# Delta rule: a head's values turned to tokens by VectorE in 32x32 blocks and a DRAM round trip, in place of TensorE transposes

## The chip, the cores and the metric

The kernel runs on one core of a Trainium2 chip. A core has five engines, each with an instruction queue of its own that it works through in order: TensorE (PE in the profile; its weight loads are PEld), VectorE (DVE), ScalarE (ACT), GpSimd (POOL) and SyncE (SP), which here does nothing but issue DMAs. Engines wait for one another through semaphores. The metric is the time of one execution on the device, in microseconds; the median of three runs is given, beside one execution that was taken with the profiler.

## The reference, cut to what matters

The program is a decoder block of three parts: a gated delta rule (16 heads of 128 channels), a cross-attention and an attention with a mixture of experts. Only the delta rule is touched. For 4 sequences of 512 tokens:

```python
q = _causal_conv(x @ Wq.T, cw_q, cb_q)        # 4 taps along the tokens, then silu
k = _causal_conv(x @ Wk.T, cw_k, cb_k)
v = _causal_conv(x @ Wv.T, cw_v, cb_v)
...
q = _l2norm(q.reshape(Bb, Ss, H, DK))
k = _l2norm(k.reshape(Bb, Ss, H, DK))
v = v.reshape(Bb, Ss, H, DV)

def step(Sstate, inputs):
    q_t, k_t, v_t, g_t, beta_t = inputs
    retrieved = jnp.einsum('bhkv,bhk->bhv', Sstate, k_t)
    error = v_t - g_t[..., None] * retrieved
    update = k_t[..., :, None] * (beta_t[..., None] * error)[..., None, :]
    Snew = g_t[..., None, None] * Sstate + update
    o_t = jnp.einsum('bhkv,bhk->bhv', Snew, q_t)
    return (Snew, o_t)
...
o = o * jax.lax.rsqrt(jnp.mean(o * o, axis=-1, keepdims=True) + EPS) * norm_w
o = o * jax.nn.silu(x @ Wg.T)
return o @ Wo.T
```

The kernel computes the scan in chunks of 128 tokens: inside a chunk a triangular matrix is inverted, and between chunks a state of 128x128 is carried.

## The kernel before, in words

The delta rule works on 32 *pairs* `m`: a sequence `b` (4 of them) and two of its heads (`HG = 2`, index `p`), 64 heads in all. All data is float32. Each pair goes through three stages, and the stages of neighbouring pairs are woven together.

- `stage1(m)` makes keys and queries. `conv` (L598 to L612) multiplies a weight by the normalized input on PE into a PSUM tile `pb` (channels in the rows, 512 tokens in the columns), then one ACT pass (L606) and three DVE passes (L609) make the convolution in a tile `cv`, and ACT's SiLU ends it (L612). For a gate (`m == 3`) there is only the SiLU, into a tile `gs` (L602). `stage1` also writes the triangular matrices to DRAM (`at_d`, L675), and reads them back as blocks (`iA`, L740).
- `stage2_inverse(m)` inverts the blocks on POOL (on DVE for the first two pairs), 62 instructions (L751, L752), and takes the result through DRAM (`t_d`, L759; `x_d`, L762) into tiles `T` and `X` (L767, L768).
- `stage2_values(m)` makes the values and the gates. For each head it runs `conv`; PE transposes the four 128x128 chunks into a PSUM tile (L799), so that tokens are in the rows; DVE multiplies by the token's factor `nr` into the tile `vn` (L801, four buffers). Beside the first head, POOL raises `rq` to a power (L804, L805) and SP writes it to DRAM (L806).
- `stage3(m)` completes the inverse (L847 to L881), then goes through the four chunks: state times keys (L899, PE), `r` = values minus the decayed product (L901, DVE, reads `v_[p]`), inverse times `r` (L908, PE; in chunk 0 the values themselves), `u` (L910, ACT), the new state (L918 PE, L923 DVE), the output (L926, L928). Then `og` (L939) multiplies the output by norm weight and gate on DVE and frees the gate's buffer.
- `output(m)` multiplies by `Wo` (L972).

The order of work is written with Python generators. A generator yields at the points where others may go on. For pair `m`, each step of `stage3(m)` is followed by one *turn* of the rest:

```python
rest.append((stage1(m + 2), 2))
...
rest.append((stage2_values(m + 1), 1))
rest.append((inversions(m, turn), 2))
...
rest = turns(*rest)
for _ in stage3(m):
    next(rest, None)
```

A turn is thus two steps of `stage1(m + 2)`, one of `stage2_values(m + 1)`, two of the inversion, and one of `output`. A head of `stage2_values` takes five steps for its values, and two for its gate; 14 in all.

DVE, ACT and POOL issue in the order in which the program traces them (`manual_schedule`). PE's and SP's order is fixed at compile time by a planner that goes by its own estimates of when each instruction will be ready. At run time every queue, SP's too, is in order: a DMA that waits holds all that stand behind it.

Of the kernel before, what the change touches and what calls it, by code (L numbers as in the profile page):

```python
# [31 lines left out]
F32 = mybir.dt.float32  # L32
BF16 = mybir.dt.bfloat16
AF = mybir.ActivationFunctionType
ALU = mybir.AluOpType
# [4 lines left out]
P = 128  # L40
B, S, D = 4, 512, 512
NT = B * S // P
TB = S // P
# [3 lines left out]
HG = 2  # L47
# [57 lines left out]
def decoder(ctx: ExitStack, tc: tile.TileContext, a: dict, out: bass.AP):  # L105
    nc = tc.nc
# [6 lines left out]
    ident = tab[:, C_ID, :]  # L113
# [3 lines left out]
    mhalf = const.tile([P, 64], F32, name="mhalf")  # L117
# [5 lines left out]
    def along(ap, n):  # L123

        return ap.unsqueeze(2).to_broadcast([P, ap.shape[1], n])
# [22 lines left out]
    def chain(*gs):  # L148
        for g in gs:
            yield from g  # L150
# [31 lines left out]
    def run(*gs):  # L182
        for g in gs:
            for _ in g:
                pass
# [17 lines left out]
    dram = ctx.enter_context(tc.tile_pool(name="dram", bufs=1, space=DRAM))  # L203
# [174 lines left out]
    with ExitStack() as st:  # L378
# [3 lines left out]
        w2 = st.enter_context(tc.tile_pool(name="a_2", bufs=2))  # L382
# [14 lines left out]
        p_b = st.enter_context(tc.tile_pool(name="a_pb", bufs=4, space=PSUM))  # L397
# [23 lines left out]
        SLOTS = 3  # L421
# [3 lines left out]
        r_d = [dram.tile([HG * TB, P], F32, name=f"r_d{n}") for n in range(SLOTS)]  # L425
# [21 lines left out]
        def blocks(d):  # L447

            f = d.rearrange("c x -> (c x)").rearrange("(n x) -> n x", x=BLK)
            return f[:, : 32 * P].rearrange("n (r t) -> n r t", r=32)[:, :, 0:32]  # L450
# [133 lines left out]
        def load_weights(m, *what, by=nc.sync):  # L584

            for n in what:
                if m < B * NHG:
                    t = (s1 if n < 2 else s2).tile([P, KD, HG * P], F32, name=f"w{n}", bufs=1)
                    by.dma_start(t, a["a_w"][m % NHG][:, n])
                    weights[m, n] = t  # L590

        def conv(b, hg, p, m, wt, dst):

            h = hg * HG + p
            xnT = seqs[b][0]
            pj = p_b.tile([P, S], F32, name="pb")
            for kd in range(KD):
                nc.tensor.matmul(pj, wt[:, kd, p * P : (p + 1) * P], xnT[:, kd, :], start=kd == 0, stop=kd == KD - 1)  # L598
                if kd == 1:
                    yield  # L600
            if m == 3:
                nc.scalar.activation(dst, pj, AF.Silu)  # L602
                yield
                return
            ac = w2.tile([P, S], F32, name="cv", bufs=5)
            nc.scalar.activation(ac, pj, AF.Identity, bias=cb[:, m, h : h + 1], scale=cw[:, m, h, 3:4])  # L606
            yield
            for j in range(1, 4):
                nc.vector.scalar_tensor_tensor(ac[:, j:], pj[:, : S - j], cw[:, m, h, 3 - j : 4 - j], ac[:, j:], ALU.mult, ALU.add)  # L609
                if j == 2:  # L610
                    yield
            nc.scalar.activation(ac if dst is None else dst, ac, AF.Silu)  # L612
            return ac
# [174 lines left out]
        def stage2_values(m):  # L788

            b, hg = divmod(m, NHG)  # L790
            nr, rq = keys[m][4:]
            wv, wg = weights.pop((m, 2)), weights.pop((m, 3))
            v_, gs = [], []
            for p in range(HG):
                t = yield from conv(b, hg, p, 2, wv, None)
                yield
                tp = p_b.tile([P, TB, P], F32, name="pb")
                for c in range(TB):
                    nc.tensor.transpose(tp[:, c, :], t[:, c * P : (c + 1) * P], ident)  # L799
                v = w2.tile([P, TB, P], F32, name="vn", bufs=4)  # L800
                nc.vector.tensor_tensor(v, tp, along(nr[:, p * TB : (p + 1) * TB], P), ALU.mult)  # L801
                v_.append(v)
                if p == 0:
                    nc.gpsimd.tensor_scalar(rq, rq, 1e-24, None, ALU.max)  # L804
                    nc.gpsimd.tensor_tensor(rq, rq, mhalf[:, 0 : HG * TB], ALU.pow)  # L805
                    nc.sync.dma_start(r_d[m % SLOTS].rearrange("c t -> (c t)").rearrange("(n k) -> n k", k=HG * TB), rq)  # L806
                yield
            load_weights(m + 1, 2)
            for p in range(HG):
                g = w2.tile([P, S], F32, name="gs", bufs=3)  # L810
                yield from conv(b, hg, p, 3, wg, g)
                gs.append(g)
            load_weights(m + 1, 3)
            pairs[m] = (v_, gs)

# [17 lines left out]
        def stage3(m):  # L833

            b, hg = divmod(m, NHG)
            xnT, beta, gam, ngam, gend, gall = seqs[b]
            kT, kd_, qg, pt, _, _ = keys.pop(m)
            Ts, Xs, ats = joined.pop(m)
            v_, gs = pairs.pop(m)
# [44 lines left out]
            t = w2.tile([P, HG, S], F32, name="rrow", bufs=1)  # L884
# [5 lines left out]
            for c in range(TB):  # L890
                cs = slice(c * P, (c + 1) * P)
                rs = []
                for p in range(HG):
                    h = hg * HG + p
                    if c == 0:
                        rs.append(v_[p][:, 0, :])
                        continue
                    pk = p_s.tile([P, P], F32, name="ps")
                    nc.tensor.matmul(pk, kT[p][:, cs], st_[p], start=True, stop=True)  # L899
                    r = small.tile([P, P], F32, name="r", bufs=3)  # L900
                    nc.vector.scalar_tensor_tensor(r, pk, ngam[:, h, c : c + 1], v_[p][:, c, :], ALU.mult, ALU.add)  # L901
                    rs.append(r)
                if c:
                    yield
                us = []
                for p in range(HG):
                    pu = p_s.tile([P, P], F32, name="ps")
                    nc.tensor.matmul(pu, Xs[p][:, c, :], rs[p], start=True, stop=True)  # L908
                    u = small.tile([P, P], F32, name="u", bufs=4)
                    nc.scalar.copy(u, pu)  # L910
                    us.append(u)
                yield
                nst = list(st_)
                for p in range(HG):
                    h = hg * HG + p
                    if c < TB - 1:
                        pn = p_s.tile([P, P], F32, name="ps")
                        nc.tensor.matmul(pn, kd_[p][:, c, :], us[p], start=True, stop=True)  # L918
                        s_ = small.tile([P, P], F32, name="state", bufs=4)
                        if c == 0:  # L920
                            nc.scalar.copy(s_, pn)
                        else:
                            nc.vector.scalar_tensor_tensor(s_, st_[p], gall[:, h, c : c + 1], pn, ALU.mult, ALU.add)  # L923
                        nst[p] = s_
                for p in range(HG):
                    nc.tensor.matmul(po[p][:, c, :], us[p], pt[p][:, c, :], start=True, stop=c == 0)  # L926
                    if c > 0:
                        nc.tensor.matmul(po[p][:, c, :], st_[p], qg[p][:, cs], start=False, stop=True)  # L928
                st_ = nst
                if 0 < c <= HG:  # L930
                    nc.gpsimd.tensor_tensor(gs[c - 1], gs[c - 1], rb[c - 1], ALU.mult)
                yield
# [150 lines left out]

        context = prepare()
        run(turns((stage2_inverse(0), 2), (chain(pair0, turns((stage1(1), 2), (stage2_values(0), 1))), 1), (itertools.islice(context, 11), 1)))
        begun[1] = stage2_inverse(1)
        for m in range(NP):
# [29 lines left out]
            if m + 1 < NP:  # L1117
                rest.append((stage2_values(m + 1), 1))
                rest.append((inversions(m, turn), 2))
# [8 lines left out]
            for _ in stage3(m):  # L1128
                next(rest, None)
# [12 lines left out]
    with ExitStack() as st:  # L1142
        keep = st.enter_context(tc.tile_pool(name="b_keep", bufs=1, reuse_waits="tile"))
        small = st.enter_context(tc.tile_pool(name="b_small", bufs=4, reuse_waits="tile"))
        p_b = st.enter_context(tc.tile_pool(name="b_pb", bufs=6, space=PSUM, reuse_waits="tile"))
# [571 lines left out]
        for i in range(NT - 1):  # L1717
            g, kind = rest_of(i), "rest_of"
            if i in (3, 7, 11):
                g, kind = chain(g, route(i - 3, 4)), "route"  # L1720
                at_e.append((i + 1.6, 2.0 if i < 11 else 0.45, enter(i - 3), "enter"))
            elif i == NT - 4:
                g, kind = chain(g, table(EARLY, "e", count, None, True, ahead)), "route"
            elif i == NT - 2:
                g, kind = chain(g, route(12, 3)), "route"
# [179 lines left out]
```

## Time and profile before

| what | value |
|---|---|
| three runs | 3327.7, 3330.07, 3330.5 us |
| median | 3330.07 us |
| the profiled execution | 3329.88 us |
| its span, first to last instruction | 3328.1 us |
| mean granted TensorE clock | 0.981 |
| instructions | 48186 |
| DMA | 476.09 MB, mean 143 GB/s |
| the delta rule's values (L801) | from 103 to 1788 us |

The span is what the trace covers; 1.8 us lie around it. A group of the profile reads: line, engine, operation, what it writes and reads with buffer numbers left out, shapes, count, then busy time in us and the mean of one in ns, then the idle time of the engine just before these instructions and what ended it. The busy time counts overlapping instructions once; the mean of one does not, so a pipelined matmul's mean is longer than the time for which it holds the engine. Two records stand for one float32 matmul, one for a float32 transpose. In a timeline, `SPq` is the issue of a DMA on SP, whose length is the issue's, not the transfer's.

### The profile page before, as it was taken

Reading aid. Unit: us, or ns where it says so; the run is one execution under the profiler, and the core shown is the slowest. Engines: PE = TensorE matmul, PEld = TensorE weight load, DVE = VectorE, ACT = ScalarE, POOL = GpSimd, SP = SyncE. Lnnn points to the kernel's source line nnn. Section 1 sums busy time; section 2 is a strip of 40 time slices with the busy share of each in tenths; the row PEclk is TensorE's granted clock in tenths of the full one; section 3 lists DMA queues with packets and bytes.
Section 4 is the critical chain, followed back from the end, with each engine's and each line's share of the span. In section 5 each row is a group of like instructions: output and inputs, shape, how many; then the busy total and the mean of one; then the engine's idle time right before and its main releaser. Section 6 shows DMA issues by size and latency. Waiting matters only on the chain. (4 is left out here: it accounts for less than half of the span.)

```text
span 3328.1 us, 48186 instructions
## 1 busy us (share of the span) xinstructions
PE 3166.4 (95%) x16015; PEld 1775.2 (53%) x16015; DVE 1831.9 (55%) x4184; ACT 1606.6 (48%) x4391; POOL 1465.7 (44%) x2780
## 2 busy tenths in 40 slices
PE   5899999999999999999998789999999999999998
PEld 3555555555555555555555445555555555555444
DVE  5665555546555556555454566656665665646211
ACT  3445555545554455545453346455555555645222
POOL 1156757676666666676765211112212221121443
PEclk8999999999999999999998799999999999999999
DMA  6343534444444434454434455556655565567454
GB/s 171 103 134 114 145 103 131 138 124 126 118 129 137 133 117 121 124 148 126 121 108 120 144 178 185 176 161 186 183 167 165 184 168 155 175 198 263 93 89 60
DMA packets 491032, 476.09 MB, mean 143 GB/s; under 512 B 225332, under 2 KB 340554, under 8 KB 490656
## 3 DMA queue, kind: packets, MB, share of 16 engines
q1 hardware_dynamic: 477616, 444.59, 45.5%
q0 software_dynamic: 11728, 25.58, 3.8%
q8 instruction: 128, 2.10, 0.3%
q10 hardware_dynamic: 1440, 2.84, 0.3%
q14 instruction: 120, 0.98, 0.1%
HBM read 411.23 MB, written 61.69 MB: 142 GB/s over the span
## 5 line engine op out<-in xcount | busy, mean ns | idle before, releaser
L598 PE MATMUL pb<-xnT,w 128*128 128x512 f32 x2048 | 958.6, 603 | 0.5 <-DVE at L674 0.2
L598 PEld LDWEIGHTS pb<-xnT,w 128*128 128x128 f32 x2048 | 364.8, 192 | 340.4 <-issue 333.5
L609 DVE SCALAR_TENSOR_TENSOR cv<-pb,pp,cv 128x510 f32<-128x510 f32 (+2 forms) x576 | 424.3, 746 | 92.7 <-ACT cv L606 79.4
L752 POOL TENSOR_TENSOR iT<-iT,iW 64x126 f32<-64x126 f32 (+22 forms) x930 | 344.7, 371 | 72.8
L1267 PE MATMUL pb<-c_q,hT 128*128 128x512 f32 x768 | 353.0, 599 | 3.3 <-DMA c_q<-in_c_wq_dram 1.6
L751 POOL TENSOR_TENSOR iW<-iA,iT 64x126 f32<-64x126 f32 (+22 forms) x930 | 321.6, 346 | 65.7 <-issue 0.2
L1186 POOL TENSOR_TENSOR rope_s<-q,tab 128x128 f32<-128x128 f32 x80 | 45.0, 563 | 481.6 <-DVE q L1297 368.3
L972 PE MATMUL pb<-wot,og 128*128 128x512 f32 x512 | 247.6, 607 | 5.5 <-DVE xa L977 4.5
L1267 PEld LDWEIGHTS pb<-c_q,hT 128*128 128x128 f32 x768 | 141.4, 192 | 157.4 <-issue 147.3
L606 ACT ACTIVATE cv<-pb,pp 128x512 f32<-128x512 f32 x192 | 148.7, 774 | 148.1 <-PE pb L598 144.2
L653 POOL TENSOR_TENSOR rk<-ss,mhalf 128x8 f32<-128x8 f32 x32 | 77.7, 2428 | 276.3 <-DVE ss L652 276.3
L977 DVE TENSOR_TENSOR xa<-pb,xa 128x512 f32<-128x512 f32 x112 | 77.1, 688 | 187.2 <-PE pb L972 187.2
L306 ACT ACTIVATE x_e<-pb,nm,x_step 128x256 f32<-128x256 f32 x256 | 141.2, 565 | 57.8 <-DVE nm L302 56.7
L1380 PE MATMUL pw<-wot,oT 128*128 128x512 f32 x344 | 162.6, 599 | 1.6 <-DVE oT L1372 1.3
L1333 PE MATMUL pb<-kT,qT 128*128 128x256 f32 (+3 forms) x576 | 163.2, 409 | 0.8 <-ACT og L1339 0.7
L705 POOL TENSOR_TENSOR qg<-qh,row 128x512 f32<-128x512 f32 x64 | 82.8, 1293 | 171.7 <-ACT qh L612 149.2
L972 PEld LDWEIGHTS pb<-wot,og 128*128 128x128 f32 x512 | 92.6, 192 | 100.2 <-issue 89.2
L612 ACT ACTIVATE qh<-cv 128x512 f32<-128x512 f32 x64 | 40.4, 631 | 212.8 <-DVE cv L609 212.8
L1782 PE MATMUL pb<-w_gu,eT 128*128 x288 | 130.3, 595 | 3.1 <-issue 3.1
L1366 ACT COPY eT<-pb 128x512 f32<-128x512 f32 x160 | 91.5, 596 | 85.2 <-PE pb L1364 84.3
L132 POOL TENSOR_TENSOR rms_r<-rsq,mhalf 128x1 f32<-128x1 f32 x48 | 27.3, 570 | 220.4 <-DVE rsq L131 220.4
L458 ACT ACTIVATE em<-em,ee 128x128 f32<-128x128 f32 x256 | 78.3, 388 | 94.5 <-POOL ee L655 81.6
(436 smaller groups left out, 6239.9 us busy)
## 6 DMA issues: line engine op xcount, KB each, us to landing
c_q<-in_c_wq_dram SPq DMA_DIRECT2D x128, 512.0 KB
w<-in_a_w_dram SPq DMA_DIRECT2D x124, 512.0 KB
wot<-in_c_wo_dram SPq DMA_DIRECT2D x86, 512.0 KB
row<-g_d SPq DMA_DIRECT2D x64, 512.0 KB
c_o<-in_c_wo_dram SPq DMA_DIRECT2D x42, 512.0 KB
at_d<-at SPq DMA_DIRECT2D x64, 256.0 KB
rrow<-r_d SPq DMA_DIRECT2D x32, 512.0 KB
T<-t_d SPq DMA_DIRECT2D x32, 512.0 KB
```

Source lines behind the costliest of these rows:

```text
L306: nc.scalar.activation(e[:, 2 * r + g, :], ps[r][:, g, :], AF.Exp, bias=nm[:, r, g : g + 1], scale=step[:, h : h + 1], accum_out=ssum[:, g ...
L598: nc.tensor.matmul(pj, wt[:, kd, p * P : (p + 1) * P], xnT[:, kd, :], start=kd == 0, stop=kd == KD - 1)
L606: nc.scalar.activation(ac, pj, AF.Identity, bias=cb[:, m, h : h + 1], scale=cw[:, m, h, 3:4])
L609: nc.vector.scalar_tensor_tensor(ac[:, j:], pj[:, : S - j], cw[:, m, h, 3 - j : 4 - j], ac[:, j:], ALU.mult, ALU.add)
L751: eng.tensor_tensor(u, A[:, i, i + 1 :].unsqueeze(2).to_broadcast([nb, n, w]), T[:, i, :w].unsqueeze(1).to_broadcast([nb, n, w]), ALU.mult)
L752: eng.tensor_tensor(T[:, i + 1 :, :w], T[:, i + 1 :, :w], u, ALU.add)
L972: nc.tensor.matmul(pw, og[p][:, c * P : (c + 1) * P], wot[:, p, :], start=p == 0, stop=p == HG - 1)
L1267: nc.tensor.matmul(pj, hT[:, kd, :], w[:, kd % 2, :], start=kd == 0, stop=kd == KD - 1)
L1333: nc.tensor.matmul(ps[:, m, k * P : (k + w) * P], qT[g][:, n + m, :], kT[:, g, j : j + w, :], start=True, stop=True)
L1366: nc.scalar.copy(eT, tp)
L1380: nc.tensor.matmul(pw, oT[:, h + m, :], w[:, m, :], start=g == 0 and h + m == 0, stop=g == 3 and h + m == 3)
L1782: nc.tensor.matmul(pg, hT[:, kd, :], w_gu[:, bass.ds(e, 1), kd, :, :], start=kd == 0, stop=kd == KD - 1)
```

## The change

The four transposes of a head on PE go, with their PSUM tile. A generator `brought` does their work for each head. VectorE transposes every 32x32 block of the head's 128x512 tile in place of its own position, so that row `32 q + j` holds token `j` of every block of 32 tokens and 32 channels of group `q`. Four DMAs, one for each group of 32 rows, write the blocks to a DRAM tile `v_d` in the order of the tokens (pieces of 512 bytes). Two turns later one DMA reads it back as the tile `vn` (2 KB a row), and two turns after that DVE multiplies it by `nr`, in place. The convolutions stand in `conv_all`, as they were, and after each of its steps the heads that have begun take one step of `brought`; the number of steps of `stage2_values` stays 14, and the second head's multiply is traced in the last of them.

The order inside `vn` is now channel group, chunk, 32 channels, so `stage3` reads a chunk of it as four pieces of 32, and `r` is written by the same instruction with its operands seen as four blocks.

```diff
-            v_, gs = [], []
-            for p in range(HG):
-                t = yield from conv(b, hg, p, 2, wv, None)
-                yield
-                tp = p_b.tile([P, TB, P], F32, name="pb")
-                for c in range(TB):
-                    nc.tensor.transpose(tp[:, c, :], t[:, c * P : (c + 1) * P], ident)
-                v = w2.tile([P, TB, P], F32, name="vn", bufs=4)
-                nc.vector.tensor_tensor(v, tp, along(nr[:, p * TB : (p + 1) * TB], P), ALU.mult)
-                v_.append(v)
...
+            v_, gs, beside = [], [], []
+
+            def brought(p, t):
+
+                x = w2.tile([P, 4, TB, 32], F32, name="vt", bufs=1)
+                nc.vector.transpose(x.rearrange("p b k i -> p k b i"), t.rearrange("p (k b j) -> p k b j", b=4, j=32))
+                d = dram.tile([P, 4, P], F32, name="v_d", bufs=4)
+                for q in range(4):
+                    nc.sync.dma_start(d[:, q, :].rearrange("(b j) x -> j b x", b=4), x[q * 32 : (q + 1) * 32].rearrange("p b k i -> p b (k i)"))
+                yield
+                yield
+                v = w2.tile([P, 4, TB, 32], F32, name="vn", bufs=4)
+                v_.append(v.rearrange("p a k i -> p k a i"))
+                nc.sync.dma_start(v.rearrange("p a k i -> p a (k i)"), d)
+                yield
+                yield
+                nc.vector.tensor_tensor(v, v, nr[:, p * TB : (p + 1) * TB].unsqueeze(1).unsqueeze(3).to_broadcast([P, 4, TB, 32]), ALU.mult)
+
+            def conv_all():
+                for p in range(HG):
+                    t = yield from conv(b, hg, p, 2, wv, None)
+                    yield
+                    beside.append(brought(p, t))
+                    if p == 0:
...
+                    yield
+                load_weights(m + 1, 2)
+                for p in range(HG):
+                    g = w2.tile([P, S], F32, name="gs", bufs=3)
+                    yield from conv(b, hg, p, 3, wg, g)
+                    gs.append(g)
+
+            for _ in conv_all():
+                for g in beside:
+                    next(g, None)
+                yield
+            run(*beside)
             load_weights(m + 1, 3)
             pairs[m] = (v_, gs)
...
-                        rs.append(v_[p][:, 0, :])
+                        rs.append(v_[p][:, 0])
...
-                    nc.vector.scalar_tensor_tensor(r, pk, ngam[:, h, c : c + 1], v_[p][:, c, :], ALU.mult, ALU.add)
+                    blocks = lambda t: t.rearrange("p (a i) -> p a i", i=32)
+                    nc.vector.scalar_tensor_tensor(blocks(r), blocks(pk), ngam[:, h, c : c + 1], v_[p][:, c], ALU.mult, ALU.add)
                     rs.append(r)
```

More of the change, by code (lines that the diff above doesn't have):

```diff
@@ L792, in stage2_values @@
             wv, wg = weights.pop((m, 2)), weights.pop((m, 3))
-            v_, gs = [], []
-            for p in range(HG):
-                t = yield from conv(b, hg, p, 2, wv, None)
-                yield
-                tp = p_b.tile([P, TB, P], F32, name="pb")
-                for c in range(TB):
-                    nc.tensor.transpose(tp[:, c, :], t[:, c * P : (c + 1) * P], ident)
-                v = w2.tile([P, TB, P], F32, name="vn", bufs=4)
-                nc.vector.tensor_tensor(v, tp, along(nr[:, p * TB : (p + 1) * TB], P), ALU.mult)
-                v_.append(v)
[L803 to L806, printed above, removed]
-                yield
@@ L808, in stage2_values @@
[L808 to L812, printed above, removed]
+            v_, gs, beside = [], [], []
[5 more added lines that the diff above has]
+                    nc.sync.dma_start(d[:, q, :].rearrange("(b j) x -> j b x", b=4), x[q * 32 : (q + 1) * 32].rearrange("p b k i -> p b (k i)"))
+                yield
+                yield
+                v = w2.tile([P, 4, TB, 32], F32, name="vn", bufs=4)
[4 more added lines that the diff above has]
+                nc.vector.tensor_tensor(v, v, nr[:, p * TB : (p + 1) * TB].unsqueeze(1).unsqueeze(3).to_broadcast([P, 4, TB, 32]), ALU.mult)
@@ new lines, in conv_all @@
+            def conv_all():
[4 more added lines that the diff above has]
+                    if p == 0:
+                        nc.gpsimd.tensor_scalar(rq, rq, 1e-24, None, ALU.max)
+                        nc.gpsimd.tensor_tensor(rq, rq, mhalf[:, 0 : HG * TB], ALU.pow)
+                        nc.sync.dma_start(r_d[m % SLOTS].rearrange("c t -> (c t)").rearrange("(n k) -> n k", k=HG * TB), rq)
+                    yield
[4 more added lines that the diff above has]
+                    gs.append(g)
```

## The prediction

> **What bounds the kernel now.** I read the page first, then the busy time by stretches, then the groups by form for the edited lines, then the timeline of one pair (from 697 to 753 us), and last who waits on SP's queue.
>
> The page, engines over the whole span:
>
> ```profile
> PE 3166.4 (95%) x16015; PEld 1775.2 (53%) x16015; DVE 1831.9 (55%) x4184; ACT 1606.6 (48%) x4391; POOL 1465.7 (44%) x2780
> ```
>
> The stretches of the delta rule's stage (columns: stretch, PE, PEld, DVE, ACT and POOL busy us with counts, granted clock, DMA share, GB/s):
>
> ```profile
> 600.00:800.00 200.00, 198.90 (x1167) 114.62 (x1165) 106.11 (x175) 100.82 (x282) 138.05 (x297) 1.00 0.48 135
> 800.00:1000.00 200.00, 196.02 (x1150) 116.07 (x1150) 117.16 (x218) 108.59 (x304) 130.54 (x279) 1.00 0.45 126
> ```
>
> From 200 to 1800 us PE is busy 97 to 99.5% at a granted clock of 1.00 (0.97 in the last stretch); DVE and ACT stand near 54%, POOL near 67%. PE sets this stage: PE time that goes comes off the end, unless another engine makes PE wait.
>
> The groups by form of the lines that go:
>
> ```profile
> L799 PE MATMUL pb<-tab,cv 128*128 128x128 f32 x256 | 42.8, 291 | 3.6 <-ACT cv L612 3.6
> L801 DVE TENSOR_TENSOR vn<-pb,nr 128x512 f32<-128x512 f32 x64 | 44.2, 691 | 72.1 <-PE pb L799 72.1
> ```
>
> The timeline around the second head's values of one pair (start, length):
>
> ```profile
> 715.55 0.60 DVE L901 SCALAR_TENSOR_TENSOR r<-ps,ngam,vn 128x128 f32<-128x128 f32 x2
> 716.27 0.61 ACT L612 ACTIVATE cv<-cv 128x512 f32<-128x512 f32 x1
> 716.94 0.66 PE L799 MATMUL pb<-tab,cv 128*128 128x128 f32 x4
> 717.43 0.61 PE L908 MATMUL ps<-r,X 128*128 128x128 f32 x4
> 717.63 0.69 DVE L801 TENSOR_TENSOR vn<-pb,nr 128x512 f32<-128x512 f32 x1 [1.48 <-PE pb L799]
> 719.02 0.92 SPq L759 DMA_DIRECT2D t_d<-iT  x2
> 721.93 0.38 SPq L767 DMA_DIRECT2D T<-t_d  x1
> 723.06 0.36 SPq L768 DMA_DIRECT2D X<-x_d  x1
> 725.08 1.17 SPq L724 DMA_DIRECT2D rq<-sr  x2
> 726.19 0.69 DVE L688 TENSOR_TENSOR pt<-pb,em 128x512 f32<-128x512 f32 x1 [0.50 <-PE pb L686]
> 730.06 0.35 SPq L589 DMA_DIRECT2D w<-in_a_w_dram  x1
> 730.58 1.41 DVE L939 SCALAR_TENSOR_TENSOR og<-po,pp,gs 128x512 f32<-128x512 f32 x2 [3.71 <-PE po L928]
> 731.37 0.60 ACT L602 ACTIVATE gs<-pb 128x512 f32<-128x512 f32 x1 [2.75 <-DVE og L939]
> ```
>
> See that PE goes from L799 to L908 after 0.49 us, that DVE has a gap from 726.88 to 730.58, and that ACT already stands behind og. A pair lasts 52.8 us (L801 of the first head starts at 699.56 and 752.35).
>
> **What goes from PE.** Four transposes a head keep PE from its next instruction 0.49 us (716.94 to 717.43; also 698.87 to 699.36 and 751.65 to 752.15). The last 512-column matmul before them starts at 716.36 and the next could follow 0.43 us later, so about 0.15 us more is PE's wait for ACT's SiLU. Pair 0 lies in the start, where PE is busy only 146 of 200 us, so I count 62 of 64 heads: 62 x 0.49 = 30.4 us certain; with all of the wait 62 x 0.64 = 39.7 us. I take half of the wait: **35 us**. One PSUM tile of L799 a head goes too; PE's waits for such tiles are small (0.5 us before all of L598), so nothing for that.
>
> **What comes to VectorE.** Two instructions in place of one a head. The multiply by `nr` now reads SBUF; the same operation, a tile times a broadcast row, is L230: 681 to 694 ns, so 0.69 us, as before. The 32x32 transpose has no row. Bounds over the same 128x512 floats: a cast, 0.41 us (L1044), and a scan, 1.21 us (L662). I take 0.69, what most one-pass rows have. DVE gains 64 x 0.69 = 44 us (26 to 77), some 2.5% of the stage (1.5 to 4.4%), on an engine with 46% free, and loses 72.1 us of waiting for L799. No PE time by itself.
>
> The Trainium skill's VectorE: DVE Perf Modes, § The three transpose paths, gives 311 ns for a 128x128 bf16 block on VectorE; four of them would be an estimated 1.24 us, and the sum would stay, with that page's estimate at the upper bound above.
>
> **The round trip.** Each head issues five DMAs on SP that were not there: four of 64 KB out, one of 256 KB back. Out: a t_d issue of 64 KB takes 0.46 us (0.92 for two), so 1.84 us. Landing: t_d's issue ends at 719.94 and T, which needs it, goes at 721.93, so 2.0 us. Read: issue 0.34 us (xi, also 256 KB from DRAM), landing 4.3 us (its issue ends at 1918.16; DVE, waiting for it, starts at 1922.49). Unhindered: 1.84 + 2.0 + 0.34 + 4.3 = **8.5 us**. In trace order the read stands two turns behind the writes, the multiply two more, and a turn is about 3.6 us (five lie between the two L801, 699.56 and 717.63).
>
> - First head: SiLU ends at 698.81, transpose done at 699.5, tile back at 708.0. The multiply's place is behind the second head's last FMA, near 715.6: 7.6 us of cover. It costs nothing while SP lets the read go by 711, thus ahead of the iA loads, which stand at 712.54.
> - Second head: transposed at 717.6, back at 726.1 at best. The multiply stands between pt (ends at 726.88) and og (730.58): it may start until 729.9. Cover: 3.8 us for queueing on SP, where t_d, x_d, T, a weight load and X take 3.0 us together. I take the read right behind X, at 723.4: lands at 728.1, og on time, **0 us**.
>
> What is moved past: T goes up to 1.84 us later on SP. L847 needs it at 730.85; 721.93 + 1.84 + 0.38 + 4.3 = 728.5, so hidden. Nothing is added to POOL's queue. Traffic: 64 x 512 KB = 33.6 MB on the 444.59 MB for which q1 took 45.5% of the engines' span, 3.4 points over the span, some 6 to 7 in a stage at 0.39 to 0.49: no bound.
>
> **The step that can make PE wait.** The first head's multiply stands right ahead of r (L901, 715.55 to 716.15), which PE needs for L908. Slack before: 717.43 - 716.15 = 1.28 us; with L799 and half the wait gone, 0.71. A push of 0.69 just fits. But the multiply reads two SBUF tensors, and DVE is stretched under POOL there:
>
> ```profile
> 64.94 0.77 DVE L751 TENSOR_TENSOR iW<-iA,iT 64x115 f32<-64x115 f32 x1
> 66.04 0.27 DVE L751 TENSOR_TENSOR iW<-iA,iT 64x110 f32<-64x110 f32 x1
> 64.18 1.38 POOL L705 TENSOR_TENSOR qg<-qh,row 128x512 f32<-128x512 f32 x1 [14.57 <-ACT qh L612]
> ```
>
> The first ends only as L705 does (65.71 and 65.56). Behind a POOL operation of 0.4 us the push is 1.1, behind L705 (1.29 at 715.78) 1.96. So PE stalls 0 to 1.25 us a pair; with the usual POOL operation on some pairs I take 0.1 x 31 = **3 us**. The Trainium skill's SBUF — State Buffer, § SBUF: two separate sides, says that a DVE operation with two SBUF inputs and a GpSimd operation that reads SBUF exclude each other for the whole instruction; the trace agrees (0.77 against 0.27 us).
>
> Start, pair 0: DVE carries an inversion there; 0 to 3 us, I take **1**.
>
> **Sum.** 35 - 3 - 1 = 31 us. The span 3328.1 becomes 3297; the profiled execution, 3329.9 with 1.8 us around the span, becomes **3299**. It lies 0.2 us from the median of the runs (3330.07), so that needs no correction. Own range of this case: 39.7 plus some 2 for waits that shrink, down to 12 where the second head's read goes behind both rq issues (726.25: lands at 730.9, og 1.0 us late) and r is late on some pairs: 3288 to 3318.
>
> **The rivals.**
>
> 1. *The second head's tile is late and og with it* (slower). SP issues in order, and the planner fixes that order. If the read falls behind the weight load of 730.06, which waits for PE, it goes at 730.4, lands at 732.9 (2.2 us after its issue, as at_d's write before iA) to 735.0 (4.3). The multiply holds DVE, og starts at 733.6 to 735.7 in place of 730.58, and behind og stand ACT's gs, the Y copies and cv, for which PE's L857 waits. ACT's cv ends at 735.77 and PE is free at about 736.4, so 0.6 us is covered. Price 2.4 to 4.5 us a pair, x 31 = 74 to 140; less the 31: near **3375** at the lower end. It decides from a stall of 31 / 31 = 1.0 us a pair: og at 732.2, a read later than 726.9, thus anywhere behind iT's issue (it ends at 726.83). For it: SP's queue stands long behind PE and POOL:
>
> ```profile
> SPq L806 <- POOL rq L805: 303.7, 28, 13.9
> SPq L589 <- PE pb L598: 147.7, 38, 12.0
> ```
>
> Against it: the read is traced a turn ahead of these loads and ready 4 us earlier. The Trainium skill's VectorE: DVE Perf Modes, § Rules for kernel authors, advises TensorE for a 128x128 transpose when PSUM will do as its destination; by that rule the change loses, and here only this wait could make it so.
>
> 2. *r is late on every pair* (no change). POOL holds the multiply each time: 1.25 x 31 = 39 us in place of 3: 3329.9 - 35 + 1 + 39 = **3335**. For it: POOL is 67% busy, and L705 starts within 0.2 us of the multiply's place. Against: L705 itself waits for ACT, and whichever starts first wins.
>
> That the change does not do what it says is hardly possible: the transposes are written out and go.
>
> **How the numbers follow.** A measurement of this kernel can tell about 0.2%, 6.7 us, from no change (3323.4 to 3336.7). The forecast 0.64, all faster. Rival 1 0.20, all slower. Rival 2 with its halves 0.16: 0.02 faster, 0.09 within, 0.05 slower. Faster 0.66, same 0.09, slower 0.25. The range from 3284 to 3350 leaves out about 0.03 below and 0.17 above, most of rival 1.
>
> **What would show it.** Right: no group of 256 at L799; PE's busy time down by some 43 us; a pair of 51.7 us in place of 52.8; DVE's transpose between 0.41 and 1.21 us; the multiply with next to no wait for a DMA; og and ACT's gs as before. Wrong: DVE's multiply waiting for vn's load by more than 1 us a pair, or r released late before L908; then PE's share falls below 97% in the stretches above. A read issued behind L589 would point to rival 1; multiplies near 1.9 us to rival 2.

## The result, and the profile after

| kernel | median | range of its runs | profiled span | mean granted clock |
|---|---|---|---|---|
| before | 3329.75 us | 3327.7 to 3330.5 | 3328.1 us | 0.981 |
| changed | 3313.91 us | 3312.34 to 3316.98 | 3310.5 us | 0.982 |

The ratio is 0.9954, with a 95% interval of 0.9940 to 0.9969: the kernel is faster by 0.46%, about half of what was forecast (3299 us). The medians differ by 15.8 us, the spans of the profiled executions by 17.6 us, where the sum had 31. Runs of one kernel scatter by 3 to 12 us, so small differences between kernels are read from the lengths of single pairs below, and not from the spans. Every ratio is against runs of the kernel before that were made beside it.

The page of the changed kernel, engines over the whole span, and the groups by form that stand where L799 and L801 stood:

```profile
PE 3134.8 (95%) x15759; PEld 1754.4 (53%) x15759; DVE 1877.9 (57%) x4248; ACT 1603.0 (48%) x4391; POOL 1487.7 (45%) x2780
```

```profile
L809 DVE TENSOR_TENSOR vn<-vn,nr 128x512 f32<-128x512 f32 x64 | 46.2, 721 | 156.4 <-DMA vn<-v_d 156.4
L798 DVE STREAM_TRANSPOSE vt<-cv 128x512 f32<-128x512 f32 x64 | 45.4, 710 | 9.7 <-ACT cv L612 7.2
```

PE has lost its 256 transposes (16015 instructions to 15759) and 31.6 us of busy time. DVE has gained 46 us, as forecast (44): its transpose takes 0.71 us, the multiply 0.72. The wait of 72.1 us for L799 is gone, and one of 156.4 us for the tile's load has come.

The same stretches of the delta rule's stage (columns as before):

```profile
600.00:800.00 200.00, 197.11 (x1159) 113.81 (x1159) 115.05 (x191) 101.28 (x289) 139.82 (x289) 1.00 0.53 151
800.00:1000.00 200.00, 194.61 (x1127) 113.62 (x1126) 119.12 (x218) 106.48 (x294) 135.69 (x285) 0.99 0.54 151
```

PE's share fell from 99.4 and 98.0% to 98.6 and 97.3%: PE waits more than before. The list of waits says for whom, changed kernel first, then before (columns: total us, count, longest):

```profile
DVE vn L809 <- DMA vn<-v_d: 156.4, 32, 7.5
ACT gs L602 <- DVE og L959: 138.5, 29, 8.5
```

```profile
ACT gs L602 <- DVE og L939: 82.7, 29, 5.7
```

32 waits: only the second heads' tiles are late, and all of them are. The first heads' never are.

To find where PE pays I measured the stretches from one pair's first `ps<-vn` matmul on PE (chunk 0) to the next pair's. A stretch bears the number of the pair at whose matmul it ends; the first pair is 0, the last 31. "Into the pair" counts from the start of this stretch. Most are alike, and I call those steady; 1, 30 and 31 lie at the ends and are left out. Nine more are not steady, and I call them passages: where a new sequence's preparation is woven in (5, 6, 13, 14, 21, 22), and where output rows are written and `x` is loaded (9, 17, 25). Two columns give what was gained or lost against before (minus is gained) by the start of the last pair, and over the whole span.

| kernel | steady | 5, 13, 21 | 6, 14, 22 | 9, 17, 25 | at the last pair | span |
|---|---|---|---|---|---|---|
| before | 52.79 | 56.31 56.30 56.30 | 57.13 57.14 57.14 | 53.94 55.18 54.27 | | |
| changed | 51.93 | 56.51 56.36 56.37 | 58.65 58.78 57.09 | 54.76 56.36 56.04 | -13.7 | -17.6 |
| e1_no_turn | 51.93 | 55.44 55.31 55.31 | 56.00 56.01 56.03 | 54.30 55.32 54.06 | -27.3 | -24.8 |
| e2_late_second | 51.93 | 55.57 55.56 55.56 | 57.06 57.09 58.72 | 54.02 54.04 54.06 | -22.6 | -21.0 |
| e3_late_first | 51.93 | 56.36 56.36 56.36 | 56.00 55.99 55.99 | 58.17 57.70 54.86 | -12.6 | -11.5 |
| e4_late_both | 51.93 | 55.31 55.44 55.43 | 56.00 56.01 56.00 | 53.72 53.74 53.73 | -28.0 | -23.1 |
| e5_read_soon | 51.93 | 55.55 55.54 55.54 | 57.06 57.10 57.09 | 54.14 55.72 55.07 | -20.5 | -21.8 |
| e6_write_twice | 52.35 to 53.49 | 56.94 57.30 57.87 | 58.84 59.07 57.86 | 55.12 56.18 58.49 | +16.7 | +13.7 |
| e7_soon_first_late | 51.93 | 55.43 55.43 55.43 | 56.00 56.00 56.00 | 54.71 55.84 54.80 | -19.9 | -20.0 |

The first two rows hold the answer. A steady pair gains 0.86 us whether its tile is late or not. The nine passages together do not gain 0.86 each: they grow by 7.2 us.

### The profile page after: what moved, and what is told of

The parts are those of the page before. It is cut to its first block, busy times and chain, and to the rows that moved or that the text cites. A ratio compares the mean times of both kernels' runs of the same rounds, so it can differ in the third digit from the quotient of the medians.

```text
span 3310.5 us, 48238 instructions
## 1 busy us (share of the span) xinstructions
PE 3134.8 (95%) x15759; PEld 1754.4 (53%) x15759; DVE 1877.9 (57%) x4248; ACT 1603.0 (48%) x4391; POOL 1487.7 (45%) x2780
## 5 line engine op out<-in xcount | busy, mean ns | idle before, releaser
L598 PE MATMUL pb<-xnT,w 128*128 128x512 f32 x2048 | 953.1, 602 | 3.4 <-DVE g_a L519 2.0
L598 PEld LDWEIGHTS pb<-xnT,w 128*128 128x128 f32 x2048 | 366.8, 192 | 355.4 <-issue 344.6
L606 ACT ACTIVATE cv<-pb,pp 128x512 f32<-128x512 f32 x192 | 148.5, 774 | 125.4 <-PE pb L598 120.2
L705 POOL TENSOR_TENSOR qg<-qh,row 128x512 f32<-128x512 f32 x64 | 91.7, 1432 | 143.1 <-ACT qh L612 131.8
L612 ACT ACTIVATE qh<-cv 128x512 f32<-128x512 f32 x64 | 40.4, 631 | 200.2 <-DVE cv L609 200.2
L809 DVE TENSOR_TENSOR vn<-vn,nr 128x512 f32<-128x512 f32 x64 | 46.2, 721 | 156.4 <-DMA vn<-v_d 156.4
L132 POOL TENSOR_TENSOR rms_r<-rsq,mhalf 128x1 f32<-128x1 f32 x48 | 27.3, 570 | 222.2 <-DVE rsq L131 222.2
```

The costliest lines, as they stand in the source:

```text
L705: nc.gpsimd.tensor_tensor(g, q, mb[p], ALU.mult)
```

## Where a steady pair keeps its 0.86 us though og is late

The changed kernel's SP in one steady pair, second head (start, length of the issue):

```profile
717.72 0.38 SPq L767 DMA_DIRECT2D T<-t_d  x1
718.20 0.58 SPq L724 DMA_DIRECT2D rq<-sr  x1
718.89 0.39 SPq L768 DMA_DIRECT2D X<-x_d  x1
719.33 1.01 SPq L724 DMA_DIRECT2D rq<-sr  x1
720.38 0.45 SPq L806 DMA_DIRECT2D vn<-v_d  x1
```

The read stands behind X and behind both `rq` issues, which the forecast had as the low end of its range, not as its value. It lands 3.6 us after its issue (the multiply starts at 724.44); over all pairs it is 3.1 to 5.5 us. In the steady pair 3, where the landing took the longest, 5.5 us, `og` comes 2.2 us later than in the same pair of before, measured from the pair's start (35.64 against 33.43), and 3.1 us later than it could (32.58 in e1_no_turn). PE doesn't mind. Timelines of PE, before and changed, each from that pair, behind the last matmul of L847 (L866 now):

```profile
299.89 5.42 PE L598 MATMUL pb<-xnT,w 128*128 128x512 f32 x12
305.24 0.31 PE L857 MATMUL pb<-Y,X 128*64 128x32 f32 x4
```

```profile
294.62 7.13 PE L598 MATMUL pb<-xnT,w 128*128 128x512 f32 x16
301.68 0.31 PE L876 MATMUL pb<-Y,X 128*64 128x32 f32 x4
```

And ACT in the changed kernel:

```profile
297.79 0.60 ACT L602 ACTIVATE gs<-pb 128x512 f32<-128x512 f32 x1 [5.80 <-DVE og L959]
...
301.13 0.26 ACT L870 COPY Y<-pb 32x128 f32<-32x128 f32 x1
301.42 0.78 ACT L606 ACTIVATE cv<-pb,pp 128x512 f32<-128x512 f32 x1
```

Two things are to be seen. What L876 needs are the Y copies, which end at 301.39; the `cv` behind them (L606) ends at 302.20, when L876 runs already. So the forecast's cover of 0.6 us, counted to `cv`, was short: in the pair of before the copies end at 303.62 and L857 starts at 305.24, 1.6 us. And the planner has put 16 records of L598 ahead of L876 where it had 12, 4 x 0.43 = 1.7 us more. Together 3.3 us, against the 3.1 that were needed: the tile's lateness just fits. In the other steady pairs of the changed kernel `og` starts between 33.7 and 35.7 us into the pair, so all of them fit.

## The experiments

The first four took the multiplies or the whole round trip out of the way.

**e1_no_turn** is the kernel before without the transposes.

```diff
-                tp = p_b.tile([P, TB, P], F32, name="pb")
-                for c in range(TB):
-                    nc.tensor.transpose(tp[:, c, :], t[:, c * P : (c + 1) * P], ident)
...
-                nc.vector.tensor_tensor(v, tp, along(nr[:, p * TB : (p + 1) * TB], P), ALU.mult)
+                nc.vector.tensor_tensor(v, t.rearrange("p (c j) -> p c j", c=TB), along(nr[:, p * TB : (p + 1) * TB], P), ALU.mult)
```

> The kernel before with the four PE transposes of a head left out and nothing put in their place: DVE multiplies the tile with channels in its rows as if they were tokens, so the values are not those of the reference. It shows what the removal is worth alone. Theory A (the gain is lost at the pairs where one sequence passes to the next, through the round trip and the multiplies): a steady pair takes 51.8 to 51.9 us as in the changed kernel, since ACT's chain and not the round trip sets that, and the pairs at the passages (5, 6, 9, 13, 14, 17, 21, 22, 25) shrink by 0.7 to 1 us each as the others do; span near 3298 (30 less than before). Theory B (at the passages ACT and DVE set the pace, and PE time saved there is worth nothing whatever replaces the transposes): steady pair 51.9, the passages no shorter than before or longer; span near 3310. Theory C (the round trip costs something in every pair): steady pair near 51.5, span near 3290.

3306.13 us, ratio 0.9930 (0.9914 to 0.9945), span 3303.3. The steady pair is 51.93 us here too, without any round trip, so 0.86 us is all that the transposes are worth, and in steady pairs the round trip is free. The passages do shrink here, by 0.9 to 1.1 us where a sequence is prepared. So the gain that the changed kernel misses there is lost to the round trip. The time is above what was expected: the ceiling itself is lower than the forecast's 35 us. And 9 and 17 do not shrink, against what was expected (54.30 and 55.32 us, before 53.94 and 55.18). In 17 `og` is held up in both kernels by DVE's wait for the `x_in` load ahead of it, 4.88 us, and starts 37.5 us into the pair before the change, not 33.4. The kernel before has no cover left there; its PE already waits for the Y copies:

```profile
1062.87 0.30 PE L857 MATMUL pb<-Y,X 128*64 128x32 f32 x2 [0.45 <-ACT Y L850]
```

**e2_late_second, e3_late_first, e4_late_both** move the multiply of the second head, of the first, and of both into the third step of the next `stage3`, behind `og`. The edit is e2's; e3 has the heads `(0,)` and e4 `(0, 1)`.

```diff
-                nc.vector.tensor_tensor(v, v, nr[:, p * TB : (p + 1) * TB].unsqueeze(1).unsqueeze(3).to_broadcast([P, 4, TB, 32]), ALU.mult)
+                if p in (1,):
+                    later.append((p, v))
+                else:
+                    nc.vector.tensor_tensor(v, v, nr[:, p * TB : (p + 1) * TB].unsqueeze(1).unsqueeze(3).to_broadcast([P, 4, TB, 32]), ALU.mult)
...
+            for p, v in later:
+                nc.vector.tensor_tensor(v, v, nr[:, p * TB : (p + 1) * TB].unsqueeze(1).unsqueeze(3).to_broadcast([P, 4, TB, 32]), ALU.mult)
```

> The changed kernel with the multiply of the second head alone moved behind og, into the third step of the next pair's last stage, so that DVE never stands in front of og waiting for the read. Theory A: pairs 9, 17 and 25 give back about 2 us each and 5, 13, 21 about 1 us each, steady pairs stay at 51.93; span 3310.5 - 9 = 3301 to 3303; the wait of ACT's gs for og falls from 138 to about 83 us. Theory B: no change, 3310. Theory C: steady pairs shorter by 0.2 to 0.4 us, span near 3292.

3309.34 us, ratio 0.9936 (0.9920 to 0.9951), span 3307.1, slower than expected but in the direction. The waits for the tile are gone and `gs`'s wait for `og` is 77.0 us, below that of before. Passages 9, 17 and 25 fall to 54.0, and 5, 13 and 21 to 55.6; 6, 14 and 22 don't. So the late second tile is what costs at six of the nine. How it costs at 9, 17 and 25, the changed kernel's DVE at passage 17 shows, and PE beside it:

```profile
1052.35 0.70 DVE L809 TENSOR_TENSOR vn<-vn,nr 128x512 f32<-128x512 f32 x1 [7.49 <-DMA vn<-v_d]
1052.97 1.40 DVE L1012 SCALAR_TENSOR_TENSOR xa<-xa,a_rs,x_in 128x512 f32<-128x512 f32 x2
1054.29 1.40 DVE L959 SCALAR_TENSOR_TENSOR og<-po,pp,gs 128x512 f32<-128x512 f32 x2
```

```profile
1057.88 0.30 PE L876 MATMUL pb<-Y,X 128*64 128x32 f32 x2 [1.52 <-ACT Y L869]
```

The read was issued at 1047.43, behind two `x` loads and two output writes (L984, L1016) on SP. The multiply waits for it with two L1012 and `og` queued behind; `og` starts 40.4 us into the pair, ACT's `gs` and Y after it, and PE stands 1.5 us. This is the chain of rival 1 (multiply, `og`, `gs`, Y, PE), at 9, 17 and 25 alone; the read stands behind the `x` loads there, not behind a weight load. At 5, 13 and 21 PE doesn't wait for Y at all. It waits further on, for DVE's `g_a`, and e2, e4 and e5 have no such wait; how the late tile leads to it was not followed. In the changed kernel at passage 5:

```profile
413.74 1.55 PE L598 MATMUL pb<-xnT,w 128*128 128x512 f32 x3 [0.66 <-DVE g_a L519]
```

> The changed kernel with the multiply of the first head alone moved into the third step of the next pair's last stage, thus out from in front of r; the second head's stays. Theory A: pairs 6 and 14 give back about 2.4 us each and 22 about 0.8, since r comes earlier and the granted clock no longer falls to 0.67 near 445 and 875 us; steady pairs stay; span 3304 to 3306. Theory B: no change, 3310.

3318.64 us, ratio 0.9962 (0.9946 to 0.9977), span 3316.6. Faster than the changed kernel was expected, and it is not: the two intervals overlap, but passages 9 and 17 are 3.4 and 1.3 us longer. The part it was made for came out: 6, 14 and 22 are 56.0. What those passages suffer from is the first head's multiply ahead of `r`. The changed kernel at passage 14:

```profile
872.90 0.68 DVE L809 TENSOR_TENSOR vn<-vn,nr 128x512 f32<-128x512 f32 x1
...
874.39 0.94 PE L686 MATMUL pb<-qh,kT 128*128 128x128 f32 x6 [1.11 <-ACT qh L612]
874.41 1.30 POOL L705 TENSOR_TENSOR qg<-qh,row 128x512 f32<-128x512 f32 x1 [5.86 <-ACT qh L612]
874.44 1.35 DVE L556 SCALAR_TENSOR_TENSOR sp_y<-sp_z,sp_y 128x64 f32<-128x64 f32 x1
...
875.72 0.60 DVE L921 SCALAR_TENSOR_TENSOR r<-ps,ngam,vn 128x128 f32<-128x128 f32 x2
876.11 0.81 PE L928 MATMUL ps<-r,X 128*128 128x128 f32 x4 [0.79 <-DVE r L921]
...
877.15 3.34 PE L598 MATMUL pb<-xnT,w 128*128 128x512 f32 x4
```

The multiply pushes five small `sp_*` operations of the next sequence back by 0.6 us, and one of them (L556) then coincides with POOL's L705 and takes 1.35 us in place of 0.23 (as in e4_late_both); the Trainium skill's SBUF — State Buffer, § SBUF: two separate sides, has such a pair exclude each other, and L556 ends at 875.79 as L705 does at 875.71. So `r` is late and PE waits 0.79 us in L928. This is the end of rival 2, at three pairs of 31, by another way: it is not the multiply that POOL holds up, but an operation that the multiply has pushed. The four records of L598 behind it then take 3.34 us instead of 1.88 (0.43 us apart); of this more below.

But in e3 the second tile lands later at 9 and 17: at passage 9 its read is issued 33.2 us into the pair (32.7 in the changed kernel) and lands 5.1 us after the issue's end (3.3), `og` starts 2.0 us later, and PE waits 2.25 us for Y. SP's order there is the same. Why the same transfer is slower was not settled; e3 shows only that a kernel with one fault mended can lose at the other.

> The changed kernel with both multiplies moved. Theory A: both gains add, span 3295 to 3299, thus faster than the changed kernel by 0.3 to 0.45% and than the kernel before by 0.9 to 1.0%. Theory B: no change, 3310. Theory C: near 3288.

3306.77 us, ratio 0.9924 (0.9910 to 0.9937), span 3305.0. All nine passages are below those of e1_no_turn, which has no round trip at all, or within 0.13 us of them, and at the last pair 28.0 us are gained. Its ratio is the lowest of the kernels that compute the whole, though e2's interval overlaps. At 9, 17 and 25 the planner has 16 records of L598 ahead of the Y matmuls here, as in e2 and the changed kernel, and 12 in e1, e5, e7 and before; so its lead over e1 there fits the planner's order and is no gain by the round trip. The span is 6 us above what was expected, 5 of it lost behind the delta rule's stage, where nothing was changed (28.0 gained at the last pair, 23.1 at the end). The other kernels drift there by -4 to +3 us in the same way; the cause stays open.

The next three ask whether it is SP's order that makes the second tile late, and what lateness costs.

**e5_read_soon** traces the second head's read one turn earlier, its multiply where it was. **e7_soon_first_late** does this and e3's edit.

```diff
-                yield
-                yield
+                for _ in range(1 if p else 2):
+                    yield
                 v = w2.tile([P, 4, TB, 32], F32, name="vn", bufs=4)
...
-                yield
-                yield
+                for _ in range(3 if p else 2):
+                    yield
```

> The changed kernel with the second head's read traced one turn earlier and its multiply in its old place; SP's order then has the read ahead of T, X and both rq issues. Theory (SP's place makes the second tile late where a passage loads SP): the read goes about 3 us earlier, the multiply's wait falls from 4.6 to 6.2 us to 1 to 3 us in steady pairs (whose length stays 51.9) and below 4 us at passages; pairs 9, 17, 25 and 31 come to about 54.05 us as in e2_late_second, pairs 6 and 14 keep their loss of some 2.6 us. Time 3306 to 3311. Rival (the read is late by the landing, not by its place, or T behind it becomes late): pairs 9, 17 and 25 stay at 54.8 to 56.4 or new waits of PE at L866 appear, time 3313 to 3330.

3310.75 us, ratio 0.9949 (0.9933 to 0.9966), span 3306.3, within what was expected. The group of the multiply and SP's queue in the pair shown above:

```profile
L809 DVE TENSOR_TENSOR vn<-vn,nr 128x512 f32<-128x512 f32 x64 | 46.6, 728 | 4.4 <-DMA vn<-v_d 4.2
```

```profile
715.21 0.39 SPq L806 DMA_DIRECT2D vn<-v_d  x1
716.38 0.38 SPq L767 DMA_DIRECT2D T<-t_d  x1
716.97 0.42 SPq L768 DMA_DIRECT2D X<-x_d  x1
717.44 1.64 SPq L724 DMA_DIRECT2D rq<-sr  x2
```

The read now goes ahead of T, 26.4 us into the pair instead of 29.4, and the wait falls from 156.4 us to 4.2. So the place on SP is what makes the tile late. In this pair the read goes 3.0 us earlier, and it also lands sooner, 2.3 us after its issue instead of 3.6; what shortens the landing was not tested. Passages 5, 13, 21 and 9 are where e2 has them. 17 and 25 are not (55.7 and 55.1 against 54.0), but where the rival had them: at 17 DVE's last L1012 waits 4.6 us for `x_in`, whose load is issued when it was in e2 and lands 1.0 us later, with the read ahead of it. `og` starts 38.1 us into the pair instead of 37.1, and the planner has 12 records of L598 in front of the Y matmuls where e2 has 16, so PE waits for Y, 0.87 us; in e2 the copies were done 0.9 us before PE came. The ratios of e5 (0.9933 to 0.9966) and of the changed kernel (0.9940 to 0.9969) can't be told apart; the passages can.

> Both faults mended in separate ways: the second head's read one turn earlier (its multiply in its old place), the first head's multiply moved behind r as in e3_late_first. Theory (two separate faults; e3 lost because the second tile was late there): pairs 6, 14 and 22 at 56.0, pairs 9, 17 and 25 near 54, no dip of the granted clock, time 3305 to 3309 as e4_late_both. Rival (moving the first head's multiply by itself costs something at the passages 9, 17 and 31): those stay near 57 to 58 us and the time near 3315 to 3319.

3310.04 us, ratio 0.9945 (0.9929 to 0.9962), span 3308.1, some 1 us above what was expected. 6, 14 and 22 are at 56.0, and 9 and 17, which e3 had at 58.2 and 57.7, are at 54.7 and 55.8: the two faults are separate, and e3's loss was the late second tile. What keeps it from e4's time is what e5 shows at 9, 17 and 25, and 6 us in pair 1 (71.2 us against 65.2), where PE waits 3.16 us for T, which the read now precedes on SP, and the granted clock then falls to 0.5; that was not followed further.

**e6_write_twice** has the second head's four writes issued twice.

```diff
                 d = dram.tile([P, 4, P], F32, name="v_d", bufs=4)
+                if p:
+                    e = dram.tile([P, 4, P], F32, name="v_e", bufs=4)
+                    for q in range(4):
+                        nc.sync.dma_start(e[:, q, :].rearrange("(b j) x -> j b x", b=4), x[q * 32 : (q + 1) * 32].rearrange("p b k i -> p b (k i)"))
                 for q in range(4):
```

> The changed kernel with the second head's four writes issued twice (the first time to a scratch that nothing reads): some 1.84 us more of SP ahead of t_d, T, X, rq and the read, in every pair. The multiply's wait in steady pairs grows from 4.6 to 6.2 us to about 6.5 to 8 us. Theory (a steady pair covers an og that is late by about 3 us, and loses beyond it, as the passages with a wait of 7.5 us do): most steady pairs lose 0 to 1 us, the passages 1 to 2 us more each: 3320 to 3345. Rival (the forecast's cover of 0.6 us behind og is right and some other slack hid it): every pair loses the full 1.8 us: 3370 or more. Rival (og is never what sets a pair, the passages lose by something else): 3313 to 3317.

3348.60 us, ratio 1.0067 (1.0048 to 1.0086), span 3341.8: slower than before, some 35 us behind the changed kernel and above the 3320 to 3345 that were expected. The waits were 5.0 to 6.5 us in the steady pairs, less than expected (4.1 to 6.2 in the changed kernel), but the cost was there. The planner's order differs again here: 12 records of L598 stand ahead of the Y matmuls, not 16, so the cover is the 1.6 us of the kernel before. With 12 records and `og` at 32.58, e1, e2, e4, e5 and e7 have pairs of 51.93; here `og` is later in every one. From the pair's start, `og` starts at 34.65, 35.15, 35.59 and 36.13 us, and the pair lasts 52.35, 52.50, 52.95 and 53.49: beyond about 35 us one for one. The changed kernel, with 16 records, has 51.93 at 35.64, and e3, with 16 as well, has 52.59 at 36.66 (pair 3). The lateness is thus free up to a threshold and then paid, and the threshold moves with the PE work that the planner has put in between. For the same reason e6 doesn't show what 1.8 us on SP cost alone: no steady `og` is later than 36.13 here, and the changed kernel at 35.64 has its Y copies done 0.29 us ahead of PE, so by an estimate from these rows 16 records would have left a loss of some 0.2 us at most. By this estimate most of what the steady pairs lose here is the planner's order.

## Why the prediction came out half

The sign and the mechanism were right: PE bounds the stage, the transposes come off the end, the round trip is hidden in the usual pair. Three terms of the sum were mis-sized. Against the 31 us of the sum, for the span of the profiled execution:

- *35 us from PE.* By the starts of PE's records in one pair (11), the first head gave 0.59 us and the second 0.63: the 0.49 of the transposes, as taken, and 0.10 and 0.14 of PE's waits for SiLU. That is 1.22 us in place of the 1.13 that I had. But 0.37 of it was lost again in the same pair, where PE comes to the product of state and keys (L899, now L918) before ACT has copied the state; the rows are below. This leaves 0.86 us a steady pair. I had counted the waits that shrink and none that would grow once PE came earlier to the next engine. 31 x 0.86 = 26.7, 8.3 less. e1_no_turn, with the same 51.93, shows this as the ceiling.
- *0 us for the second head's tile.* I put the read right behind X, and it came behind `rq`. In steady pairs that was free, by a cover larger than the 0.6 us I had: 3.3 us, of which 1.7 came by the planner's new order. That part was luck; with the 1.6 us of the old order the steady pairs pay, as e6_write_twice shows. At six passages it was not, and there I had priced nothing: all of the cover had been read from one steady pair. Against e4_late_both, pairs 5, 13, 21 and 9, 17, 25 lose 9.0 us. This is the step that failed worst; next to it stands the 35 us, put too high by 8.3.
- *3 us for r pushed by the first head's multiply.* In steady pairs it was free: the multiply keeps to 0.72 us on average, nowhere near the 1.9 that rival 2 needed. At 6, 14 and 22 it lost 6.5 us against e4_late_both: 1.1 at each, and the rest by a lower clock at two.

The rows for the first of these, from pair 11, the kernel before and the changed one:

```profile
703.34 0.42 ACT L921 COPY state<-ps 128x128 f32<-128x128 f32 x2
703.69 0.67 PE L899 MATMUL ps<-state,kT 128*128 128x128 f32 x4
```

```profile
697.17 0.42 ACT L941 COPY state<-ps 128x128 f32<-128x128 f32 x2
697.48 0.71 PE L918 MATMUL ps<-state,kT 128*128 128x128 f32 x4 [0.17 <-ACT state L941]
```

The pairs start at 697.14 and 690.98, so the copy ends 6.6 us into the pair in both; ACT works from 0.4 us up to it without a break, and PE can't come to the product any sooner.

On the other side the start gained 4 us by pair 0 (I had 1 lost; e5, e6 and e7 gain 3.5 to 4.5, e1 to e4 1.5 to 2.7, so what gains it is not shown), and after the stage another 3.9 came, unsettled as in e4. That such gains of 9 us offset a part of the losses is luck: the sum has no term for them. What remains, 1.5 us lost, is scattered, most of it over pairs 1, 23 and 30: 31 - 8.3 - 9.0 - 3.5 + 5 + 3.9 - 1.5 = 17.6.

One of the signs that were to show the forecast wrong came, and misled: the multiply waits 4.9 us a pair for the load, and the steady pairs lose nothing by it. PE's share didn't fall below 97%, and PE's busy time fell by 31.6 us, not by some 43.

Rival 1 was priced at 2.4 to 4.5 us a pair for every pair. Its chain is real, and in e6_write_twice it reaches the steady pairs, with a cover that the planner's order has made smaller; the changed kernel stands just within the threshold. The 64 KB writes took 1.73 to 2.98 us for four issues (median 1.77; 1.84 taken), the read's landing 3.1 to 5.5 us (median 3.7; 4.3 taken), the transpose 0.71 (0.69): no usual price of a single operation was off enough to matter.

The Trainium skill's VectorE: DVE Perf Modes, § Rules for kernel authors, prefers TensorE for a 128x128 transpose when PSUM can take it. Here the measurement goes the other way (0.9924 in e4_late_both): PE sets the stage and DVE is at 57%, and the transfer hides.

## What to carry to other kernels

When work is taken from the bounding engine, what it gains in a usual iteration is its hold on the engine less the waits that grow behind it; count the second with the first. Read the cover of a new transfer at the loop's irregular iterations, where other DMAs and other VectorE work are woven in, not at a usual one: here some 20 usual pairs had 3 us of cover, half of it by an order that the planner happened to choose, and nine others lost 15.5 us against the best placement. And place an instruction that waits for a DMA behind the work that others wait for: both multiplies moved behind `og` (e4_late_both) made the round trip free in the steady pairs and at all nine passages.

## What was not expected of the hardware

PE's granted clock fell to half behind two short waits. The changed kernel by stretches of 5 us around passage 14, whose timeline is above (the third column from the end is the granted clock):

```profile
870.00:875.00 5.00, 3.89 (x16) 2.01 (x15) 4.79 (x11) 2.54 (x4) 0.59 (x1) 1.00 0.28 50
875.00:880.00 5.00, 4.21 (x13) 2.47 (x13) 4.83 (x12) 1.72 (x4) 4.15 (x12) 0.67 0.48 133
880.00:885.00 5.00, 5.00 (x38) 3.13 (x38) 3.91 (x10) 2.47 (x7) 3.04 (x6) 0.99 0.67 139
```

In stretches of 2 us it is 0.87, 0.50 and 0.78 from 875.2 on. PE had waited 1.11 us before L686 and 0.79 us before L928, and the four records of L598 behind them took 3.34 us instead of 1.88; the passage took 58.78 us instead of 57.1. It isn't certain to happen: of passages 6, 14 and 22 of the changed kernel, e2_late_second, e5_read_soon and e6_write_twice, twelve in all, which have these same two waits to within 0.03 us, four had the drop (6 and 14 of the changed kernel, 22 of e2, 14 of e6) and eight kept a clock of 1.00. Where one wait of 1.11 us remained (e4_late_both) none had it. In all four the loss of clock adds up to 3.4 us at half speed (at passage 14 of the changed kernel 0.13, 0.50 and 0.22 missing in three stretches of 2 us make 1.7 us of full clock).

The Trainium skill's TensorE: Matmul & The Clock Gate, § What's actually happening, tells of a window of some 3.4 us that runs freely, after which the clock is set to a half or to full by how busy PE was. The length agrees, and a free-running window would explain why equal waits are caught in one passage and not in another. Its condition for the half, an idle window, does not agree: PE stood 1.9 us here. What decides it was not tested.
